# The last pair's 3x3 convolution by four products for two columns, first statistics ahead of the other weights, and a new order in the last layers

## The chip, the cores and the metric

The kernel runs on one core of a Trainium2 chip. The metric is device time in microseconds (us), the median of several executions. A profile is taken of one further execution. The engines are TensorE (PE, matmuls; its weight loads are listed as PEld), VectorE (DVE), ScalarE (ACT), GpSimd (POOL) and SyncE (SP, which here only issues DMAs). All data are 32-bit floats; every matmul of the program is recorded as two MATMUL instructions.

## What is computed

Four residual layers on x of shape (8, 64, 128, 128), each of the form x = x + layer(groupnorm(x)) with 32 groups of two channels:

```python
x = x + _L0_conv_ref(_gn(x), ...)   # 3x3 "adder" convolution: relu(b - sum |patch - w|)
x = x + _L1_conv_ref(_gn(x), ...)   # per channel: silu and a cubic spline
x = x + _L2_conv_ref(_gn(x), ...)   # Haar transform, convolutions, gelu, inverse transform
x = x + _L3_conv_ref(_gn(x), ...)   # nearest of 512 embeddings of 64 channels, per pixel
```

Layer 2 makes four half-size images of each image (256 channels of 64x64), transposes them, and applies a depthwise 3x3 convolution, a 1x1 convolution, a 3x3 convolution (256 to 256 channels), gelu and the inverse transform. Layer 3 takes, for every pixel, the embedding row with the smallest squared distance.

## The kernel before

Two images make a pair: 64 channels of each fill the 128 partitions. Four pairs are worked through. The first layer (`layer0`) is by far the longest; it makes |x - w| tiles on ACT and DVE and sums them over channels on PE (L691). While it runs for pairs 1 to 3, the layers 2 and 3 of the pair before run beside it (`layer2_beside`, `layer3_beside`), a little at every step. `layer0` issues PE, ACT and DVE instructions in an order written out by hand. Everywhere else a scheduler orders each engine's queue: program order is the priority, and an instruction is taken when the scheduler believes its inputs and buffers ready. At run time every queue, SP's of DMAs too, is worked strictly in the order chosen.

**Setup** (`setup`, L193 to L362) prepares all weights. For layer 2 it transposes the 3x3 weights (L304), multiplies them by the 1x1 weights (wp, L318) so that both convolutions become one 3x3 convolution w2 of shape 128 x 4 x 9 x 2 x 128, and stores it to DRAM (L321). gp (L335) and gam hold what the 1x1 bias gives through the 3x3 taps; `edge` makes the small tensors that correct it at the image's borders. After setup, `run` calls `raw_norm(0)`: eight tiles of pair 0 are loaded with three buffers (L403), their statistics are taken (L419), the group norm is formed, the first chunk of x is loaded into x0 (L500) and normalized (L485). Then `layer0` begins.

**The last pair** has no layer 0 to hide behind: its layers 1, 2 and 3 run alone at the end, in eight chunks of 16 image rows.

`layer1` loads its data, and, for the last pair, w2 from DRAM into SBUF in four parts (L799).

`layer2` works a chunk in these steps. `transform` forms the four Haar images on DVE (L840 to L846). `border` copies border rows between neighbouring chunks on POOL (L833, L834), for the Haar images and for the depthwise result. `depthwise` makes nine taps for each of four channel groups k on DVE (L857 the first tap, L859 the other eight). `convolve`, once for each half of the output channels (oab), multiplies nine taps x four k x two images on PE (L873), each a 64 x 128 weight by 64 x 512 columns; the two images use the upper and the lower half of the PE rows. Border corrections are small matmuls (L877). gelu goes over the 1024 columns on ACT (L879). `inverse` of the chunk before, between the two convolves, makes four positions on PE (L888), which DVE adds to x (L890), and takes statistics. The loop keeps the depthwise work one chunk ahead; a chunk can be convolved only when the depthwise result of the next chunk has given it its border row.

`layer3` works a chunk by normalizing it (L485), squaring it on ACT (L926), summing squares over channels on PE (px, L929, 16 matmuls with two columns each), and then for each of 16 rows and both images: the products with the embeddings on PE (L938), ACT's distance part t (L941), DVE's difference and maximum (L944) and its index (L946), and a gather of the embedding rows by POOL (L947). Each row's gathered values are then transposed on PE (q, L955); after four rows DVE adds them to x (L958). The chunk is stored at its end.

Of the kernel before, what the change touches and what calls it, by code (L numbers as in the profile page):

```python
# [100 lines left out]
class Net:  # L101
    def __init__(self, ctx, tc, x, w0, b0, coef, sbase, ssp, bias1, dw_w, dw_b, pw_w, pw_b, cv_w, cv_b, embed, out):
# [9 lines left out]
        self.x_of = [self.dram.tile([P, H * W], F32, name=f"x{n}_dram") for n in range(3)]  # L112
        self.setup(w0, b0, coef, sbase, ssp, bias1, dw_w, dw_b, pw_w, pw_b, cv_w, cv_b, embed)
# [6 lines left out]
    def setup(self, w0, b0, coef, sbase, ssp, bias1, dw_w, dw_b, pw_w, pw_b, cv_w, cv_b, embed):  # L120
# [66 lines left out]
        with tc.tile_pool(name="setup", bufs=1) as sp, tc.tile_pool(name="setup_ps", bufs=2, space=PSUM) as pp:  # L187
# [13 lines left out]
            for n in range(len(PLANS)):  # L201
# [7 lines left out]
                nc.vector.tensor_tensor(self.b0[:, n], ws, braw, ALU.add)  # L209

# [112 lines left out]


# [39 lines left out]
    def edge(self):  # L364
# [14 lines left out]
        for n in range(2):  # L379
# [8 lines left out]
            nc.vector.tensor_tensor(self.edge_r[n][:, HW2 - 1 : HW2], sums[:, 1:2], one[:, row[2] : row[2] + 1], ALU.subtract)  # L388

# [308 lines left out]
    def layer1(self, mr, stats, nxt):  # L698
# [3 lines left out]
        with ExitStack() as ctx:  # L702
# [49 lines left out]
            for n in range(2 * NCH):  # L752
# [44 lines left out]
                if n in range(4, 12, 2) and nxt is None:  # L797
                    k = n // 2 - 2
                    nc.sync.dma_start(out=self.w2[:, k], in_=self.w2_dram[:, k])  # L799
# [4 lines left out]
    def layer2(self, mr, stats):  # L804

# [7 lines left out]
        with ExitStack() as ctx:  # L813
            sp = ctx.enter_context(tc.tile_pool(name="l2", bufs=1))
            pp = ctx.enter_context(tc.tile_pool(name="l2_ps", bufs=2, space=PSUM))
            pi = ctx.enter_context(tc.tile_pool(name="l2_pi", bufs=1, space=PSUM))
# [6 lines left out]
            def padded(name, bufs, j):  # L823
                t = sp.tile([P, 4, G + 2, S + 2], F32, name=name, tag=name, bufs=bufs)
                nc.gpsimd.memset(t[:, :, :, 0 : S + 2 : S + 1], 0.0)
                if j == 0:
                    nc.gpsimd.memset(t[:, :, 0, 1 : S + 1], 0.0)
                if j == NCH - 1:
                    nc.gpsimd.memset(t[:, :, G + 1, 1 : S + 1], 0.0)
                return t  # L830

            def border(above, below):
                nc.gpsimd.tensor_copy(above[:, :, G + 1, 1 : S + 1], below[:, :, 1, 1 : S + 1])  # L833
                nc.gpsimd.tensor_copy(below[:, :, 0, 1 : S + 1], above[:, :, G, 1 : S + 1])  # L834

            def transform(j):
                t = padded("sub", 2, j)
                xv = self.x[j]
                s, d = (sp.tile([P, R, S], F32, name=n) for n in ("hs", "hd"))
                nc.vector.tensor_tensor(s, xv[:, :, 0:W:2], xv[:, :, 1:W:2], ALU.add)  # L840
                nc.vector.tensor_tensor(d, xv[:, :, 0:W:2], xv[:, :, 1:W:2], ALU.subtract)
                at = (slice(1, G + 1), slice(1, S + 1))
                nc.vector.scalar_tensor_tensor(t[:, 0, at[0], at[1]], s[:, 0:R:2], m4, s[:, 1:R:2], ALU.add, ALU.add)
                nc.vector.tensor_tensor(t[:, 1, at[0], at[1]], s[:, 0:R:2], s[:, 1:R:2], ALU.subtract)
                nc.vector.tensor_tensor(t[:, 2, at[0], at[1]], d[:, 0:R:2], d[:, 1:R:2], ALU.add)
                nc.vector.tensor_tensor(t[:, 3, at[0], at[1]], d[:, 0:R:2], d[:, 1:R:2], ALU.subtract)  # L846
                return t

            def depthwise(j, sub):
                t = padded("dw", 3, j)  # L850
                for k in range(4):
                    out = t[:, k, 1 : G + 1, 1 : S + 1]
                    for n, (di, dj, w) in enumerate(taps):
                        v = sub[:, k, di : di + G, dj : dj + S]
                        wt = dws[:, k, w : w + 1]
                        if n == 0:
                            nc.vector.tensor_scalar(out, v, wt, self.dwb[:, k : k + 1], ALU.mult, ALU.add)  # L857
                        else:
                            nc.vector.scalar_tensor_tensor(out, v, wt, out, ALU.mult, ALU.add)  # L859
                return t  # L860

            def convolve(j, dw, oab):
                ps = pp.tile([P, 2, G, S], F32, name="ps")
                ends = [(slice(0, G), slice(0, S, S - 1), self.edge_c)]
                if j == 0:
                    ends.append((0, slice(0, S), self.edge_r[0]))
                if j == NCH - 1:
                    ends.append((G - 1, slice(0, S), self.edge_r[1]))
                for n, (di, dj, w) in enumerate(taps):
                    for k in range(4):  # L870
                        for i, rows in enumerate(images):
                            v = dw[rows, k, di : di + G, dj : dj + S]
                            nc.tensor.matmul(ps[:, i], self.w2[rows, k, w, oab, :], v, start=(n == 0 and k == 0), stop=(n == 8 and k == 3))  # L873
                    if n == 0:
                        for r, c, e in ends:
                            for i, rows in enumerate(images):
                                nc.tensor.matmul(ps[:, i, r, c], self.gam[rows, oab, :], e[rows], start=False, stop=False)  # L877
                g = sp.tile([P, 2, G, S], F32, name="g", tag="g", bufs=4)
                nc.scalar.activation(g.rearrange("p i r c -> p (i r c)"), ps.rearrange("p i r c -> p (i r c)"), AF.Gelu, bias=self.b2c[:, oab : oab + 1])  # L879
                return g  # L880

            def inverse(j, gs):
                py = pi.tile([P, 4, G, S], F32, name="py")
# [420 lines left out]
```

## Time and profile before

| | us |
|---|---|
| median of 3 runs | 19244.84 (19237.88 to 19248.91) |
| the profiled execution: time / span | 19248.76 / 19247.0 |
| PE busy | 18582.4 (97%) |
| DVE busy | 17869.9 (93%) |
| ACT busy | 17302.3 (90%) |
| POOL busy | 2775.6 (14%) |
| granted PE clock, mean | 0.977 |

Where the stages lie in the span (us from its start):

| stage | from | to |
|---|---|---|
| setup (its last ACT instruction ends) | 0 | 98.6 |
| raw tiles, statistics and x0 of pair 0 | 98 | 133.4 |
| layer 0 of all pairs, with the rest beside it | 133.4 | 17913 |
| last pair, layer 1 | 17913 | 18172 |
| last pair, layer 2 (first L873 matmul at 18237.02) | 18172 | 18804 |
| last pair, layer 3 | 18804 | 19247 |

Durations of the rows that the change touches, from the profile's groups (mean of one, ns): L873 597, L859 744, L857 569, L888 605, L890 689, L879 1114, L938 1017, L929 353, L955 420, L944 678, L946 684, L947 958. Matmuls overlap, two with 64 rows each run side by side, and DVE's instructions overlap at their ends, so that the distance from one start to the next is shorter than these means; where that matters it is read from starts in the trace.

How to read it: a busy engine is not an engine at its peak. The chain of waits follows what ended last back through what released it; the windows give busy times, the granted clock (1.00 is full) and the DMA share for a stretch of time. An engine's idle time counts only where that engine, or one that waits for it, is the bound of the stage.

### The profile page before, as it was taken

Reading aid. Unit: us, or ns where it says so; the run is one execution under the profiler, and the core shown is the slowest. Engines: PE = TensorE matmul, PEld = TensorE weight load, DVE = VectorE, ACT = ScalarE, POOL = GpSimd, SP = SyncE. Lnnn points to the kernel's source line nnn. Section 1 sums busy time; section 2 is a strip of 40 time slices with the busy share of each in tenths; the row PEclk is TensorE's granted clock in tenths of the full one; section 3 lists DMA queues with packets and bytes.
Section 4 is the critical chain, followed back from the end, with each engine's and each line's share of the span. In section 5 each row is a group of like instructions: output and inputs, shape, how many; then the busy total and the mean of one; then the engine's idle time right before and its main releaser. Section 6 shows DMA issues by size and latency. Waiting matters only on the chain.

```text
span 19247.0 us, 328577 instructions
## 1 busy us (share of the span) xinstructions
PE 18582.4 (97%) x145850; PEld 5795.2 (30%) x145850; DVE 17869.9 (93%) x13785; ACT 17302.3 (90%) x6401; POOL 2775.6 (14%) x1698
## 2 busy tenths in 40 slices
PE   8999999999999999999999999999999999999898
PEld 2333233233233222222223222222232322222343
DVE  8999999989999999998999999998899999999837
ACT  7999999889999999988999999998999999999603
POOL 0000000000000344200000034420000004441005
PEclk9999999999999999999999999999999999999996
DMA  1000000121111000021111100002011110000101
GB/s 52 6 11 10 6 12 8 43 63 37 36 33 37 20 20 27 26 73 35 34 41 35 33 15 24 24 28 82 28 33 38 35 33 19 23 22 16 59 1 35
DMA packets 412639, 584.02 MB, mean 30 GB/s; under 512 B 64080, under 2 KB 309456, under 8 KB 385744
## 3 DMA queue, kind: packets, MB, share of 16 engines
q1 hardware_dynamic: 355408, 497.90, 8.6%
q0 software_dynamic: 55808, 65.11, 1.9%
q8 instruction: 1142, 18.71, 0.4%
q14 instruction: 281, 2.30, 0.0%
HBM read 439.55 MB, written 123.25 MB: 29 GB/s over the span
## 4 chain that ended last, share of the span: by engine, by line
PE 54%; DVE 27%; issue 9%; ACT 8%; DMA 1%; POOL 0%; SPq 0%; DVEq 0%; ACTq 0%; POOLq 0%
PE ps L691 39%; DVE buf L624 12%; DVE buf L628 9%; ACT buf L622 7%; PE cv L1066 5%; PE pa L787 2%; PE pb L787 2%; PE ps L873 2%; DVE dw L1043 1%; DVE ix L1193 1%; DVE nd L1191 1%; PE ps L938 1%; DVE x L624 1%; PE py L1089 1%; PE pd L1179 1%
## 5 line engine op out<-in xcount | busy, mean ns | idle before, releaser
L691 PE MATMUL ps<-buf,sel 128*32 128x512 f32 x116336 | 13032.1, 598 | 358.4 <-DVE buf L628 233.4
L622 ACT ACTIVATE buf<-buf,w 128x4096 f32<-128x4096 f32 x1980 | 7212.9, 3708 | 305.9 <-PE ps L691 299.5
L622 ACT ACTIVATE buf<-x,w 128x4096 f32<-128x4096 f32 x1938 | 7044.5, 3708 | 376.5 <-PE ps L691 290.8
L691 PEld LDWEIGHTS ps<-buf,sel 128*32 128x32 f32 x116336 | 3642.9, 110 | 9338.4 <-issue 7867.1
L624 DVE TENSOR_SCALAR buf<-buf,w 128x4096 f32<-128x4096 f32 x1795 | 4162.7, 2357 | 193.7 <-PE ps L691 192.9
L624 DVE TENSOR_SCALAR buf<-x,w 128x4096 f32<-128x4096 f32 x1558 | 3640.1, 2367 | 284.3 <-PE ps L691 274.5
L628 DVE SCALAR_TENSOR_TENSOR buf<-buf,w,buf 128x2048 f32<-128x2048 f32 x1262 | 2913.5, 2349 | 23.0
L628 DVE SCALAR_TENSOR_TENSOR buf<-x,w,buf 128x2048 f32<-128x2048 f32 x1072 | 2475.3, 2349 | 19.7
L1194 POOL DMA_INDIRECT g<-in_L_conv_embed_weight,ix x768 | 1825.6, 2377 | 2849.3 <-issue 1432.4
L602 POOL DMA_DIRECT2D y<-in_x x480 | 608.3, 2072 | 9442.6 <-ACT y L589 6467.9
L1066 PE MATMUL cv<-dw,w2s 64*128 64x512 f32 x6912 | 1655.2, 607 | 3.3 <-issue 3.3
L622 ACT ACTIVATE x<-buf,w 128x4096 f32<-128x4096 f32 x396 | 1468.6, 3709 | 60.8 <-PE ps L691 60.7
L691 PE MATMUL ps<-x,sel 128*32 128x512 f32 x10832 | 1302.8, 595 | 27.1 <-DVE x L628 18.9
L1066 PEld LDWEIGHTS cv<-dw,w2s 64*128 64x128 f32 x6912 | 628.0, 186 | 1025.4 <-issue 1012.0
L624 DVE TENSOR_SCALAR x<-buf,w 128x4096 f32<-128x4096 f32 x281 | 660.2, 2349 | 24.4 <-PE ps L691 24.2
L691 PEld LDWEIGHTS ps<-x,sel 128*32 128x32 f32 x10832 | 352.6, 110 | 849.1 <-issue 742.7
L1043 DVE SCALAR_TENSOR_TENSOR dw<-sub,dws,dw 128x512 f32<-128x512 f32 (+2 forms) x768 | 574.9, 749 | 10.6
L873 PE MATMUL ps<-dw,w 64*128 64x512 f32 x2304 | 525.5, 597 | 29.4 <-DVE dw L859 20.4
L1191 DVE CUSTOM_DVE_ANT_0 nd<-pd,t 128x512 f32<-128x512 f32 x768 | 520.0, 677 | 30.5 <-ACT t L1181 30.4
L1193 DVE FIND_INDEX8 ix<-best,nd 128x8 uint32<-128x512 f32 x768 | 526.1, 685 | 0.1
L776 DVE TENSOR_TENSOR r<-r,r 128x1024 f32<-128x1024 f32 x384 | 455.0, 1219 | 76.1 <-ACT r L775 76.1
L1179 PE MATMUL pd<-embT,xn 64*128 64x512 f32 x1536 | 491.4, 650 | 30.0 <-DVE best L1191 29.6
(220 smaller groups left out, 7961.3 us busy)
## 6 DMA issues: line engine op xcount, KB each, us to landing
w2s<-w_dram SPq DMA_DIRECT2D x576, 192.0 KB
xd<-x_dram SPq DMA_DIRECT2D x256, 256.0 KB
x<-x_dram SPq DMA_DIRECT2D x56, 1024.0 KB
raw<-in_x SPq DMA_DIRECT2D x32, 1024.0 KB
x_dram<-y SPq DMA_DIRECT2D x512, 64.0 KB
out<-x SPq DMA_DIRECT2D x32, 1024.0 KB
y<-in_x POOLq DMA_DIRECT2D x480, 64.0 KB, 4.2
x_dram<-x SPq DMA_DIRECT2D x24, 1024.0 KB
```

The source lines that it names most:

```text
L622: nc.scalar.activation(ab, tap(j, ts[0]), AF.Abs, bias=w[:, ts[0] : ts[0] + 1], scale=-1.0)
L624: nc.vector.tensor_scalar(ab, tap(j, ts[0]), w[:, ts[0] : ts[0] + 1], None, ALU.max)
L628: nc.vector.scalar_tensor_tensor(at, tap(j, t, h), w[:, t : t + 1], at, ALU.max, ALU.add)
L691: nc.tensor.matmul(at, sel[:, M - 1 - m : 3 * M - 1 - m], rhs, start=(n == first[p]), stop=(n + 1 == first[p + 1]))
L787: nc.tensor.matmul(to[images[i], q, :], dspl[:, k, ws[i], :], cubes[i][:, cols], start=(p == 0), stop=stop)
L873: nc.tensor.matmul(ps[:, i], self.w2[rows, k, w, oab, :], v, start=(n == 0 and k == 0), stop=(n == 8 and k == 3))
L1043: nc.vector.scalar_tensor_tensor(out, v, wt, out, ALU.mult, ALU.add)
L1066: nc.tensor.matmul(ps[:, i], weights[r, w // 3, :], v, start=(k == 0 and n == 0), stop=(k == 3 and n == 8))
L1179: nc.tensor.matmul(ps, xns[j][at, r, :], self.embT[at, :], start=True, stop=True)
L1191: nc.vector.tensor_tensor_reduce(nd, ps, t, 1.0, -FAR, ALU.subtract, ALU.max, mx[:, 0:1])
L1193: nc.vector.max_index(ix, mx, nd)
L1194: nc.gpsimd.indirect_dma_start(out=g[:, img, :], out_offset=None, in_=self.embed, in_offset=bass.IndirectOffsetOnAxis(ap=ix[:, 0:1], axis=0),)
```

## The change

**Setup.** The statistics of pair 0, the load of x0 and its normalization move from `run` into `setup`, to just behind the first layer's weights; x0 is allocated before setup. Behind the store of w2, setup computes u2 from it and stores that to DRAM too (128 x 2 x 4 x 4 x 3 x 128). `edge` makes two more small tensors, negated borders. The load of w2 into SBUF during layer 1 goes.

**Layer 2 of the last pair.** The three taps along the image's columns are replaced by a scheme that forms two neighbouring output columns from four products instead of six. Its input side v (four combinations of columns, made on DVE from the depthwise result) has half the columns; the weights u2 are combinations of the three taps. Four products m0 to m3 are accumulated over k and three row taps, each with 256 columns for each image; the outputs are m0 + (m1 + m2) for even and (m1 - m2) - m3 for odd columns, formed by one ACT copy and four DVE operations before gelu. The weights of each product are loaded from DRAM as they are needed (four buffers). The first depthwise tap goes to ACT. A chunk's Haar rows now reach two rows into the next chunk, so that a chunk's depthwise result needs no row from the next one. PSUM is divided anew: three buffers of two banks for products (before: two) and two of one bank for the inverse (before: one of four).

**Layer 3.** Chunk j + 1 is normalized and its squares are summed when row 6 of chunk j is due, its sums taken at row 12; the four transposes and the add of a group of rows come six rows later than its last row.

```diff
             nc.sync.dma_start(out=self.w2_dram, in_=w2)
+            self.u2_dram = self.dram.tile([P, 2, 4, 4, 3, P], F32, name="u2_dram")
+            for k in range(4):
+                u = sp.tile([P, 2, 4, 3, P], F32, name="u2", tag="u2")
+                g = [w2[:, k, 3 * dj : 3 * dj + 3].rearrange("p d o n -> p o d n") for dj in range(3)]
+                nc.scalar.copy(u[:, :, 0], g[0])
+                nc.scalar.copy(u[:, :, 3], g[2])
+                nc.vector.tensor_tensor(u[:, :, 1], g[0], g[2], ALU.add)
+                nc.vector.tensor_tensor(u[:, :, 2], u[:, :, 1], g[1], ALU.subtract)
+                nc.vector.tensor_tensor(u[:, :, 1], u[:, :, 1], g[1], ALU.add)
+                nc.vector.tensor_scalar(u[:, :, 1:3], u[:, :, 1:3], 0.5, None, ALU.mult)
+                for o in range(2):
+                    nc.sync.dma_start(out=self.u2_dram[:, o, :, k], in_=u[:, o])
...
+            pp = ctx.enter_context(tc.tile_pool(name="l2_ps", bufs=3, space=PSUM))
+            pi = ctx.enter_context(tc.tile_pool(name="l2_pi", bufs=2, space=PSUM))
...
+                        if n == 0:
+                            nc.scalar.activation(out, v, AF.Identity, bias=self.dwb[:, k : k + 1], scale=wt)
+                        else:
+                            nc.vector.scalar_tensor_tensor(out, v, wt, out, ALU.mult, ALU.add)
+                d = [t[:, :, :, n : n + S - 1 : 2] for n in range(4)]
+                v = sp.tile([P, 4, 4, G + 2, S // 2], F32, name="v", bufs=2)
+                nc.vector.tensor_tensor(v[:, :, 0], d[0], d[2], ALU.subtract)
+                nc.vector.tensor_tensor(v[:, :, 1], d[1], d[2], ALU.add)
+                nc.vector.tensor_tensor(v[:, :, 2], d[2], d[1], ALU.subtract)
+                nc.vector.tensor_tensor(v[:, :, 3], d[1], d[3], ALU.subtract)
+                return v
...
+                for m in range(4):
+                    if m % 2 == 0:
+                        pair = pp.tile([P, 2, 2, G, S // 2], F32, name="m")
+                    ps = pair[:, :, m % 2]
+                    u2 = sp.tile([P, 4, 3, P], F32, name="u2", tag="u2", bufs=4)
+                    nc.sync.dma_start(out=u2, in_=self.u2_dram[:, oab, m])
                     for k in range(4):
+                        for di in range(3):
                             for i, rows in enumerate(images):
+                                nc.tensor.matmul(ps[:, i], u2[rows, k, di, :], v[rows, k, m, di : di + G, :], start=(k == 0 and di == 0), stop=(k == 3 and di == 2))
...
+                m1, a, b = (sp.tile([P, 2, G, S // 2], F32, name=n) for n in ("m1", "ma", "mb"))
+                nc.scalar.copy(m1, ms[1])
+                nc.vector.tensor_tensor(a, ms[2], m1, ALU.add)
+                nc.vector.tensor_tensor(b, m1, ms[2], ALU.subtract)
+                nc.vector.tensor_tensor(g[:, :, :, 0:S:2], ms[0], a, ALU.add)
+                nc.vector.tensor_tensor(g[:, :, :, 1:S:2], b, ms[3], ALU.subtract)
...
+            for j in range(NCH):
                 done = dw
+                if j + 1 < NCH:
+                    transform(j + 1)
+                    dw = depthwise(j + 1)
+                gs = [convolve(j, done, 0)]
+                if late is not None:
+                    inverse(*late)
+                gs.append(convolve(j, done, 1))
+                late = (j, gs)
             inverse(*late)
...
+            for n in range(NCH * R + LATE):
+                j, r = divmod(n, R)
+                if j + 1 < NCH and r in (6, 12):
+                    (prepare if r == 6 else take_squares)(j + 1)
+                if j < NCH:
+                    nearest(j, r)
+                if n >= LATE + 3 and (n - LATE - 3) % 4 == 0:
+                    add(*divmod(n - LATE - 3, R))
```

## The prediction

> **What bounds the kernel now.** I read the chain of waits first, then the windows by stage, then the groups and waits of the stages that the change touches. Nearly all of the span (137 to 17913 us) is the first layer with the other pairs' layers beside it, and no instruction in it changes. Three stretches at the two ends do change, and the chain runs through all three.
>
> The start, from the chain of waits (start us, us, what):
> ```profile
> 85.04 7.93 PE gp L335 x36
> ...
> 97.96 4.68 DMA raw<-in_x
> ...
> 116.95 13.80 DMA x<-in_x
> ...
> 130.85 2.56 DVE x L485
> ...
> 133.48 3.72 ACT buf L622
> ...
> 137.25 22.87 PE ps L691 x192
> ```
> All weights are prepared first (to 98.6); only then come pair 0's raw tiles, their statistics and the first chunk of x, so that the first matmul of layer 0 starts at 137.25.
>
> The last pair's layer 2, from the chain there and from the windows (us; busy time of PE, PEld, DVE, ACT, POOL; granted clock; DMA):
> ```profile
> 18234.49 2.48 POOL dw L833
> 18237.02 14.81 PE ps L873 x56
> 18252.22 30.97 PE ps L873 x144
> 18283.31 27.57 PE ps L873 x128
> ```
> ```profile
> 18400.00:18600.00 200.00, 200.00 (x918) 87.03 (x916) 83.34 (x128) 5.65 (x6) 4.94 (x14) 1.00 0.00 1
> ...
> 18980.00:19034.00 54.00, 50.45 (x114) 20.70 (x114) 45.31 (x135) 23.30 (x34) 30.96 (x33) 0.56 0.13 40
> ```
> From 18237 to 18786 PE never rests, and DVE has half its time free: the 3x3 convolution is the bound. A convolve is 72 products, each recorded as two 512-column matmuls, the two images side by side: 144 records in 30.97 us, so 72 slots of 0.43 us (0.427 over the 288 records from 18321.5 to 18383.1). PE starts only at 18237 because two chunks must be depthwise-convolved before the first border is whole. The second row is one chunk of layer 3: DVE 45.3 of 54 us. Its idle time there, by the waits of that chunk:
> ```profile
> DVE nd L944 <- PE ps L938: 4.6, 1, 4.6
> DVE x L958 <- PE q L955: 4.1, 4, 1.3
> ```
> The 4.6 is PE doing the sums of squares of the next chunk (px, 6.9 us) ahead of products; the 4.1 are four adds whose transposes wait for a row's gather.
>
> **Part 1, the first statistics ahead of the other weights.** The chain from 97.96 to 133.48 (raw loads, statistics, x0, normalize) leaves; what stays is the weight chain, 38.8 (cvn lands) to 98.6, 59.8 us, then the first ACT tile 3.72. New at the front of SP's queue are pair 0's raw loads and x0, with their waits on the statistics (eight tiles, 2.5 us of DVE each); cvn stands behind them. If cvn still lands at 38.8, layer 0 starts at 102.3: 35 us won. If all raw and x0 traffic goes first (97.96 to 130.75, so 32.8 us, from 16.3 on, then cvn's 5.75), cvn lands at 55 and layer 0 starts at 118.5: 19 won. The u2 stores add 6.3 MB beside w2's 4.7 MB, which took 12.5 us (85.47 to 97.96), and layer 0's buffers may lie under w2 and u2: last u2 about 4 us after the last w2, then two stores together about 15 us, 104.5 instead of 98.6, so 6 less. Another 8 us go if pair 1's three raw tiles (3 MB), hoisted already now, go first too. The ends are 35 won and, with a late SP wait on top, 5 lost; I take **18 won**, near the later arrival, since program order puts the raw tiles first. The u2 arithmetic (per k two ACT copies and four DVE operations of 768 to 1536 columns; 0.58 us for 512 on ACT, 1.21 for 1024 on DVE) lies beside wp matmuls of 8 us per k, where DVE is idle; without that cover it would cost 16 us.
>
> **Part 2, layer 2.** Removed per convolve: 72 products of 512 columns. Added: 4 x 12 x 2 = 96 products of 256 columns, so 96 slots. What a slot costs hangs on the weight loads, which now come twice as often. Nearest row by columns: gp, 128x256, new weights in each of 36 records in 7.93 us, 0.22 us each. Nearest by tiling: the border matmuls of 64 rows with 16 or 64 columns, their loads one after the other:
> ```profile
> 18757.75 0.19 PEld L877 LDWEIGHTS ps<-edge_c,gam 64*128 64x128 f32 x1 [0.24 <-issue]
> 18757.75 0.18 PEld L873 LDWEIGHTS ps<-dw,w 64*128 64x128 f32 x1
> 18757.86 0.19 PEld L877 LDWEIGHTS ps<-edge_r,gam 64*128 64x128 f32 x1
> 18757.86 0.19 PEld L873 LDWEIGHTS ps<-dw,w 64*128 64x128 f32 x1
> 18757.97 0.19 PEld L877 LDWEIGHTS ps<-edge_r,gam 64*128 64x128 f32 x1
> ```
> Both row groups load at the same moment, every 0.11 us, less than the 0.213 of a 256-column slot. Ends: 0.213 (half of 0.427) and 0.40 (0.213 + 0.19, nothing overlapped). I take 0.22, by gp. The Trainium skill speaks against this: "TensorE: Matmul & The Clock Gate", Part 3, says that a weight load overlaps running matmuls only if its row group differs, and the same page's rule for loads (columns / 1.2) gives 107 ns for 128 columns. By that a slot would be 0.32, a convolve 31 us and the whole 19187. The gp row, full array and 0.22 a record, does not follow it.
>
> Convolve: 96 x 0.22 = 21.1, and four border slots of 0.11, 21.6 us. Sixteen: 16 x (30.96 - 21.6) = 149.8 won. The inverse held PE for 4 x 1.87 = 7.5 us a chunk; with two py buffers four positions of 4 slots x 0.427 = 6.8: 7 x 0.7 = 5 won. A chunk on PE is 2 x 21.6 + 6.8 = 50 us.
>
> Does DVE keep up? Pitches from its timeline: 32 taps of 0.664 = 21.2 (the first tap of each k goes to ACT, which is idle); hs/hd and sub in two parts 6.6 with the halo copy; v, four operations of 1280 columns at 1.13 per 1024, 5.7; combining, 8 x 0.69 = 5.5; adds 2.8; statistics 2.5. Sum 44 against PE's 50: DVE fits, tightly. Three m buffers give the combining about 10 us (half a convolve) before PE needs a bank back. In the first round they don't suffice: DVE is in chunk 1 for 33 us while PE is done with the first convolve after 21.6; 4 us lost there, and I allow 6 for waits like it.
>
> Start of the layer: scales at 18181.6, the second part of transform about 2 us, the first ACT tap 0.7, then 32 taps over 9 rows, 0.664 x 576/512 = 0.75 each, 23.9, and v 5.7: 18214.4 instead of 18237.0, **22.6 won**. Tail: after the last convolve, one ACT copy and four DVE operations, 3.3 lost. Weights: 64 x 2 loads of 786 KB, 6.3 MB per 50 us or 126 GB/s, alone on SP's queue then, with four buffers (over 40 us ahead); the start moved 391 GB/s, so they are hidden. If not, PE waits for them directly. The w2 loads that layer 1 loses stood beside a PE with 20.00 of 20 us busy: nothing. The two edge tiles: three DVE operations of 0.15 us, hidden in the setup. Layer 2: 149.8 + 5 + 22.6 - 10 - 3.3 = **164 won**.
>
> **Part 3, layer 3.** The transposes come six rows later, so that the 4.1 us per chunk of waits for gathers go: 8 x 4.1 = 33. The px burst stays as one block, and with it the 4.6. PE is late next: at clock 0.56 to 0.59 a row of products takes 2.07 us, 16 x 2.07 + 6.9 + 16 x 0.42 = 46.7 per chunk against DVE's 45.3, and four transposes now stand in one block of 1.7 us ahead of products. Ends: 70 won (all 8.7 us of DVE idle per chunk) and 20 lost (four uncovered blocks, 4 x 1.7 = 6.8 for 4.1 saved). I take **30 won**. On the clock the skill (same page, Part 1) says that PE drops to half rate after an idle window of 3.4 us and returns after a busy one. If fewer waits kept it at full rate, px would halve and up to 8 x 3.5 = 28 us more would go; the 0.59 in every chunk, with PE 92% busy, says that it mostly doesn't.
>
> **Sum**, against the profiled execution's 19248.76 (span 19247.0): 18 + 164 + 30 = 212, so 19036.8. That execution stands 3.9 above the median of the three, so the forecast is **19033**.
>
> **Rivals.** (a) DVE's order holds PE back: 44 of 50 us leaves little room, and depthwise of the next chunk stands ahead of the combining in program order. With 60 us per chunk, 8 x 10 = 80 less: 19113. For it: DVE did the chunks ahead in one block from 18183 to 18270. Against it: the adds of the inverse stood between such blocks where their data came.
> (b) Strict program order: DVE does 33 us of the next chunk, then combining, adds, combining behind PE; 66 us a chunk, 128 less: 19161.
> (c) All gaps close, start 35 and layer 3 70: 57 more, 18976. For it: DVE alone needs only 45.3 a chunk, and cvn could land as now.
> (d) Slower: weight loads are not overlapped in the new slots, 0.40 each. Convolve 38.9, 16 x 17.3 = 277 lost: 19310. It decides from 0.36 a slot on (212 / 16 / 96 = 0.14 above 0.22). Against it are gp and the border loads.
> (e) The change does not do what it says: the new waits (u2, m buffers, v) eat what the products save, PE idles a third of layer 2, and the time stays within 0.2% (about what a measurement can tell from no change) of 19245.
>
> **How the numbers follow.** Forecast 0.66 (19033, own range 18990 to 19080 from the ends of the start and of layer 3), (a) 0.14, (b) 0.05, (c) 0.09, (d) 0.03, (e) 0.03. Faster by over 0.2%: 0.66 + 0.14 + 0.05 + 0.09 = 0.94; within: 0.03; slower: 0.03. The range takes in (a) and (c), 18975 to 19115; (b), (d), (e) and some tails, about 2 in 10, stay out.
>
> **What would show it.** Part 1: first layer-0 matmul near 119, raw loads before cvn in SP's queue. Part 2: 192 records of 256 columns in 21 us, first at about 18196 (18214 less 18), PE without gaps from chunk 2 on, layer 3 beginning near 18622. A slot over 0.25 proves (d)'s mechanism, PE idle before m matmuls with DVE as releaser (a) or (b). Part 3: no DVE wait on q, still one of 4 to 5 us on ps per chunk, some 50 us a chunk. The prediction fails if DVE becomes the bound of layer 2, or if PE at half clock becomes that of layer 3.

## The result, and the profile after

The changed kernel takes 19155.08 us (19149.18 to 19157.30), the kernel before 19244.84: a ratio of 0.9953, 95% interval [0.9943, 0.9964]. The gain is 90 us where 212 were forecast, and the time lies above the whole range. The profiled execution took 19149.18, its span is 19147.4 us. By stages, each read from the first instruction of the next in the two traces (us):

| stage | before | changed | difference | forecast |
|---|---|---|---|---|
| to the first matmul of layer 0 | 137.25 | 143.70 | +6.4 | -18 |
| from there to the last add of layer 0 | 17774.7 | 17764.8 | -9.9 | 0 |
| last add to the first Haar operation of layer 2 (mostly layer 1) | 257.9 | 259.1 | +1.2 | 0 |
| layer 2 | 634.3 | 554.5 | -79.9 | -164 |
| layer 3 | 442.9 | 425.4 | -17.5 | -30 |
| span | 19247.0 | 19147.4 | -99.6 | -212 |

No code of the second row changes. Over the fourteen traces of this study, all with the same code there, it took 17761 to 17780 us, so a difference of 10 says nothing, and small effects below are read from their own stage and not from the total.

Lines of the changed kernel: layer 0's matmul is L722 and its ACT tile L653; in layer 2 the products m are L918, v L900 to L903, the taps L897, the combination L932 to L935, gelu L937, the inverse py L946 and its add L948; in layer 3 px is L985, ps L997, nd L1003, the transposes q L1016, their add L1018.

**The start.** The chain of waits of the changed kernel (start us, us, what):
```profile
26.53 10.71 DVE stats L450 x18
...
38.32 7.64 SPq L233
...
62.00 5.43 DMA cvn<-in_L_conv_cv_w
...
114.17 15.84 DMA u_dram<-u
...
134.55 5.27 DMA u_dram<-u
139.93 2.42 ACT buf L653
```
Raw loads and x0 no longer stand between the weights and layer 0, as meant. But the statistics and SP's first small load behind the raw loads (cf, L233) now stand ahead of the convolution's weights, which come late (the last load of cvn is issued at 67.4, before at 38.8). From these the chain runs on to the end, there twice through a store of u2: the last of four sets of u2 can be formed only when the store of an earlier one has left their only buffer, and that store stands behind the 4.7 MB one of w2. Layer 0's first ACT tile waits for the second store, because its buffer lies where u2 was.

**Layer 2.** The windows of the changed kernel (us; busy time and, in brackets, instructions of PE, PEld, DVE, ACT, POOL; granted clock; DMA share; GB/s), two chunks in the steady state, the last chunks, and one chunk of layer 3:
```profile
18348.00:18412.00 64.00, 49.69 (x402) 38.10 (x400) 39.41 (x61) 6.28 (x8) 0.61 (x1) 0.87 0.31 99
18412.00:18475.00 63.00, 51.73 (x438) 40.71 (x438) 39.62 (x59) 6.29 (x8) 0.61 (x1) 0.92 0.32 101
18570.00:18640.00 70.00, 70.00 (x594) 54.23 (x592) 23.33 (x32) 4.62 (x5) 0.00 (x0) 1.00 0.38 120
18843.00:18895.00 52.00, 39.29 (x110) 17.24 (x112) 43.84 (x133) 22.73 (x33) 30.39 (x32) 0.65 0.14 41
```
Before, PE was busy 200 of 200 us here. Now neither PE nor DVE is full in a chunk of 63 to 67 us, while at the end, where no depthwise work is left, PE is full again. Two engines that both rest may be waiting for each other. PE's waits over layer 2 (us in total, times, longest):
```profile
PE py L946 <- DVE x L948: 59.6, 4, 27.4
PE m L918 <- issue: 31.4, 2, 18.6
...
PE py L946 <- ACT g L937: 2.0, 1, 2.0
```
93 us of waits behind its first product (the 28.1 for the first v, left out, belong to the layer's start). "Issue" means that the trace names no releaser. What DVE does meanwhile, from its timeline in one chunk (start us, us, instruction, and in brackets the idle time before it and what ended it):
```profile
18366.21 0.69 DVE L932 TENSOR_TENSOR ma<-m,m 128x512 f32<-128x512 f32 x1 [18.22 <-PE m L918]
...
18368.61 1.48 DVE L900 TENSOR_TENSOR v<-dw 128x1280 f32<-128x1280 f32 x1
...
18375.24 21.33 DVE L897 SCALAR_TENSOR_TENSOR dw<-sub,dws,dw 128x512 f32<-128x512 f32 x32 [0.95 <-ACT dw L895]
...
18402.04 0.68 DVE L932 TENSOR_TENSOR ma<-m,m 128x512 f32<-128x512 f32 x1
...
18404.43 1.28 DVE L948 TENSOR_TENSOR x<-x,py 128x512 f32<-128x512 f32 x2
```
DVE has worked ahead until both buffers of v are full, idles 18.2 us for the second convolve to end, then does the combination, the next v, 32 taps and the Haar operations in one block, 36 us long. Only behind that block come the next combination and the adds of the inverse, for which PE has meanwhile stopped.

A product's cost was as forecast (start us, us, x records of 256 columns):
```profile
18682.49 15.79 PE L918 MATMUL m<-v,u 64*128 64x256 f32 x144
```
15.79 / 72 = 0.219 us a slot (the two images side by side), 21.06 for the 96 of a convolve.

**Layer 3.** DVE's waits there, changed kernel:
```profile
DVE nd L1003 <- PE ps L997: 49.7, 13, 6.3
...
DVE x L1018 <- PE q L1016: 3.7, 1, 3.7
```
Before, these two stood at 32.3 us (7 times) and 34.7. The waits for gathered rows are gone but one; the stall at each px burst but the first (4.9) has grown from 4.6 to 6.3 us, and a wait of 0.9 to 1.9 us just ahead of it has joined it.

### The profile page after: what moved, and what is told of

Read it like the earlier page. It is cut to its first block, busy times and chain, and to the rows that moved or that the text cites. A ratio compares the mean times of both kernels' runs of the same rounds, so it can differ in the third digit from the quotient of the medians.

```text
span 19147.4 us, 330733 instructions
## 1 busy us (share of the span) xinstructions
PE 18332.0 (96%) x146698; PEld 5818.3 (30%) x146698; DVE 17951.2 (94%) x13918; ACT 17340.8 (91%) x6457; POOL 2778.2 (15%) x1663
## 4 chain that ended last, share of the span: by engine, by line
PE 53%; DVE 28%; issue 10%; ACT 8%; DMA 1%; SPq 0%; POOL 0%; DVEq 0%; ACTq 0%; POOLq 0%
PE ps L722 39%; DVE buf L655 12%; DVE buf L659 9%; ACT buf L653 7%; PE cv L1139 5%; PE pa L818 2%; PE pb L818 2%; DVE dw L1116 1%; DVE nd L1264 1%; DVE ix L1266 1%; DVE dw L897 1%; PE py L1162 1%; DVE x L655 1%; ACT t L1254 1%; PE pd L1252 1%
## 5 line engine op out<-in xcount | busy, mean ns | idle before, releaser
L722 PE MATMUL ps<-buf,sel 128*32 128x512 f32 x116336 | 13030.5, 597 | 371.1 <-DVE buf L659 234.2
L653 ACT ACTIVATE buf<-buf,w 128x4096 f32<-128x4096 f32 x1980 | 7213.9, 3710 | 301.8 <-PE ps L722 295.3
L653 ACT ACTIVATE buf<-x,w 128x4096 f32<-128x4096 f32 x1938 | 7046.2, 3710 | 347.0 <-PE ps L722 288.0
L722 PEld LDWEIGHTS ps<-buf,sel 128*32 128x32 f32 x116336 | 3625.9, 110 | 9365.5 <-issue 7898.4
L653 ACT ACTIVATE x<-buf,w 128x4096 f32<-128x4096 f32 x396 | 1468.9, 3709 | 59.3 <-PE ps L722 59.3
L722 PE MATMUL ps<-x,sel 128*32 128x512 f32 x10832 | 1303.0, 594 | 27.1 <-DVE x L659 18.5
L722 PEld LDWEIGHTS ps<-x,sel 128*32 128x32 f32 x10832 | 350.8, 110 | 851.1 <-issue 747.5
L1252 PE MATMUL pd<-embT,xn 64*128 64x512 f32 x1536 | 490.1, 650 | 29.1 <-DVE best L1264 28.7
L1254 ACT ACTIVATE t<-esq_half,xsq 128x512 f32<-128x512 f32 x768 | 510.8, 717 | 3.1 <-DVE best L1264 3.1
```

The source lines that it names most:

```text
L653: nc.scalar.activation(ab, tap(j, ts[0]), AF.Abs, bias=w[:, ts[0] : ts[0] + 1], scale=-1.0)
L722: nc.tensor.matmul(at, sel[:, M - 1 - m : 3 * M - 1 - m], rhs, start=(n == first[p]), stop=(n + 1 == first[p + 1]))
L1252: nc.tensor.matmul(ps, xns[j][at, r, :], self.embT[at, :], start=True, stop=True)
L1254: nc.scalar.activation(t, self.esq_half, AF.Identity, bias=xsqs[j][:, n : n + 1])
```

## Experiments

**Layer 2: VectorE's order, the buffers, or the weights?** The work ahead becomes a generator (`steps`) and is taken in pieces, two of them ahead of each add in `inverse`; buffers and work stay as they are.
```diff
+            ctx.enter_context(tc.manual_schedule(engines={ET.PE, ET.Activation, ET.DVE}))
...
             for j in range(NCH):
+                ahead, v = steps(j + 1), vs.pop(j)
+                ms = convolve(j, v, 0)
+                take(ahead, 16)
+                gs = [combine(ms, 0)]
+                if late is not None:
+                    inverse(*late, ahead)
+                ms = convolve(j, v, 1)
+                take(ahead, 40)
+                gs.append(combine(ms, 1))
```


> The changed kernel, with layer 2's order on TensorE, ScalarE and VectorE written out: the depthwise taps of the next chunk are cut into pieces, and each combination of four products and each addition of the inverse stands between two pieces instead of behind the whole block. The work, the two buffers of v, the three of the products and the streamed weights stay as they are. In the changed kernel layer 2 took 554.5 us (18167.6 to 18722.0), two steady chunks 67 and 62.7 us. Theory 'order' (PE's 121 us of idle time in that layer all end with a VectorE instruction that stood behind some 30 us of work for a later chunk): a steady chunk falls to PE's own 50 to 53 us, PE's waits on the additions fall from 59.6 us to under 15, the two unnamed stalls of 12.8 and 18.6 us go, and the layer takes 455 to 480 us, 75 to 100 less. Rival 'buffers' (two buffers of v and three of the products are too few, whatever the order): the chunk stays at 60 us or more, and the layer loses under 20 us. Rival 'weights' (the streamed weights come late, which the two stalls without a named releaser could be): the two stalls stay, the layer takes 520 us or more.

Layer 2 took 458.3 us, 96 less, and the whole 19057.5. (6 of the 96 only moved: the first Haar operation comes 265.2 us after the last add of layer 0, not 259.1. From that add to layer 3 it is 90.) A window of it, and PE's waits on adds:
```profile
18300.00:18400.00 100.00, 97.54 (x846) 77.93 (x844) 87.39 (x129) 12.80 (x16) 3.88 (x2) 1.00 0.38 123
```
```profile
PE py L950 <- DVE x L953: 6.6, 6, 1.1
```
A chunk is 51.2 us (from one convolve's first border matmul, 18356.94, to the same one a chunk later, 18408.16), and DVE is busy 87 of 100 us where it had 40 of 63. With the buffers unchanged, "buffers" is out.

The same with only DVE's order written out, `engines={ET.DVE}`:

> As the kernel with layer 2's order written out, but for VectorE's alone: TensorE's and ScalarE's orders are left to the scheduler. With all three written out layer 2 fell from 554.5 to 458.3 us. Theory 'VectorE's order' (only the position of the combinations and additions in VectorE's queue mattered): 455 to 475 us here as well. Rival 'all three' (it took TensorE's or ScalarE's order too, say a gelu or a first tap behind a copy that waits): over 490 us.

Layer 2 took 452.1 us, PE 50.00 busy of 50 in six windows in a row. With the queues of the other two engines left to the scheduler, VectorE's order in its queue is enough. (Layer 3 took 440.4 us in that run, which is taken up below.)

The weights loaded once:
```diff
+            u2s = []
...
-                    u2 = sp.tile([P, 4, 3, P], F32, name="u2", tag="u2", bufs=4)
-                    nc.sync.dma_start(out=u2, in_=self.u2_dram[:, oab, m])
+                    if len(u2s) < 4:
+                        u2s.append(sp.tile([P, 4, 3, P], F32, name=f"u2_{m}"))
+                        nc.sync.dma_start(out=u2s[m], in_=self.u2_dram[:, oab, m])
+                    u2 = u2s[m]
```


> The changed kernel, but layer 2's convolution loads its transformed weights only once, for the four products of the first output half, and uses these for both halves and all eight chunks: 60 of the 64 loads on SP's queue are left out (the second half's output is then of the wrong weights). Rival 'weights': the stalls of 12.8 and 18.6 us in layer 2 that name no releaser go, 31 us or more off its 554.5. Theory 'order': nothing in layer 2 moves by more than 5 us, since both stalls end 0.2 to 0.4 us after the combination's third instruction, which reads the product's buffer that is wanted.

Layer 2 took 554.5 us, unmoved. (This kernel leaves out the weights of the second output half.) With the loads out of the way the trace also names the releaser of the two stalls, DVE's combination (g, L938 in this kernel):
```profile
PE py L950 <- DVE x L952: 59.5, 4, 27.3
PE m L922 <- DVE g L938: 31.4, 2, 18.6
```
So PE waited there for a product's buffer that the combination had still to read, behind DVE's taps, and streaming the weights cost nothing here.

**The start: the stores, and the move.**
```diff
-            nc.sync.dma_start(out=self.w2_dram, in_=w2)
...
-                u = sp.tile([P, 2, 4, 3, P], F32, name="u2", tag="u2")
+                u = sp.tile([P, 2, 4, 3, P], F32, name="u2", tag="u2", bufs=2)
...
                 for o in range(2):
                     nc.sync.dma_start(out=self.u2_dram[:, o, :, k], in_=u[:, o])
+            nc.sync.dma_start(out=self.w2_dram, in_=w2)
```


> The changed kernel, with two buffers instead of one for the transformed weights in the setup, and the 4.6 MB store of the old weights put behind their stores on SP's queue. In the changed kernel the first matmul of layer 0 stands at 143.70 us, the setup's own last ScalarE instruction ends at 125.8, and VectorE and ScalarE wait 11.6 and 8.3 us on the stores of u. Theory 'store' (the single buffer's stores, queued behind the large one, end the start's chain): the first matmul comes at 129 to 132 us, some 12 to 14 us earlier, and all that follows moves by as much. Rival 'weights late' (the chain is set by the weights' loads, which the statistics' loads push back from 38.8 to 67.4 us, and the stores only fill a wait that is there anyway): first matmul within 4 us of 143.70.

The first matmul came at 134.65, 9.1 us earlier, not 12 to 14. ACT's timeline in this kernel shows why:
```profile
125.59 0.60 ACT L381 ACTIVATE esq_half<-ep 128x512 f32<-128x512 f32 x1 [1.93 <-PE ep L379]
130.88 21.74 ACT L651 ACTIVATE buf<-x,w 128x4096 f32<-128x4096 f32 x6 [4.69 <-DMA u_dram<-u]
```
One store still stands between, and ACT waits 4.7 us for it. The span was 19147.1, as if nothing had been won: the middle happened to take 8 us more. The second half of the expectation, that all that follows moves as much, fell with that.

The statistics back behind the setup, u2 kept:

> The changed kernel, but with the first pair's statistics, its first chunk and that chunk's normalization back where they were, behind the setup; the transformed weights and the rest of the change stay. Theory 'the move pays, the transformed weights take it back': before the change the first matmul of layer 0 stood at 137.25; the transformed weights' two copies, four additions and stores come on top of that chain and cost 12 to 20 us, so it stands at 150 to 157 here, 6 to 13 us later than with the statistics ahead (143.70). Rival 'the move costs' (loads of the weights 28.7 us later, and nothing won): first matmul at 143 us or earlier. The middle of the run (the end of layer 0 in each pair, relative to the first) gained about 10 us in the changed kernel though none of its code was changed; if that is a matter of chance between executions, it takes another value here and in the other runs of this call.

The first matmul came at 150.07. So u2 cost 12.8 us of the old start (137.25), and the move won 6.4 of it back (143.70; the other seven kernels with the same setup have 143.9 to 146.3, so 4 to 6). With the statistics behind, the stretch that ends the start is again theirs (SP, then ACT):
```profile
112.56 18.45 SPq L430 DMA_DIRECT2D raw<-in_x  x8
```
```profile
146.30 7.32 ACT L649 ACTIVATE buf<-x,w 128x4096 f32<-128x4096 f32 x2 [42.08 <-DVE x L512]
```

**Layer 3: the gathers or the burst?** First, layer 3's old code in the changed kernel:

> The changed kernel with layer 3 as it was before: the squares' sums at the head of each chunk, the transposes in the program beside their own row. Part 3 alone is undone. If part 3 is independent of the rest, layer 3 goes from 425.4 us back to 441 to 445 and layer 2 stays at 554.5; if the 17.5 us came from something else (the clock that layer 2 leaves behind), layer 3 stays below 435.

446.5 us, with layer 2 at 555.5: by this trace and the kernel before, part 3 by itself is worth some 17 to 21 us. (Against the 440.4 above it would be 6; the last section comes back to this scatter.) Then TensorE's order in layer 3 as the program has it:
```diff
+            ctx.enter_context(tc.manual_schedule(engines={ET.PE}))
             xns, pxs, xsqs, gs = {}, {}, {}, {}
```


> The changed kernel with TensorE's order of layer 3 as the program writes it: four transposes at a time, six rows and more behind their gathers, and the 32 small matmuls px still in one burst. In the changed kernel's profile a transpose stands beside each row, waits 3.65 to 4.22 us on the gather just ahead of each px burst, and VectorE then waits 6.3 us on ps, about once a chunk (44.9 us in all). Theory 'gather' (the transposes that wait take away the lead with which TensorE enters the burst): the wait on ps shrinks to 0 to 3 us a chunk and layer 3 takes 395 to 412 us. Rival 'burst' (7 us of px are longer than any lead that four product buffers allow): the wait stays at 4 to 6 us a chunk, layer 3 at 413 to 425.

A miss for both theories: 468.6 us, 43 longer. Waits of DVE, and of PE:
```profile
DVE xsq L990 <- PE px L986: 62.3, 7, 9.1
DVE nd L1004 <- PE ps L998: 17.8, 9, 4.2
```
```profile
PE px L986 <- ACT sq L983: 56.2, 6, 12.1
```
The wait on ps did fall, but the program places px directly behind the square that it reads, and in that place PE holds everything back for ACT. The scheduler had moved px to a later place. The experiment brought in a wait of its own and decides nothing. So px was spread, from row 6 on, two of its sixteen at each row:
```diff
-                if j + 1 < NCH and r in (6, 12):
-                    (prepare if r == 6 else take_squares)(j + 1)
+                if j + 1 < NCH:
+                    if r == 4:
+                        prepare(j + 1)
+                    if r == 15:
+                        take_squares(j + 1)
                 if j < NCH:
                     nearest(j, r)
+                    if j + 1 < NCH and 6 <= r < 14:
+                        sum_squares(j + 1, 2 * (r - 6), 2 * (r - 5))
```


> As the kernel with TensorE's order written out, and the px matmuls of the next chunk besides spread over eight rows, four at each. VectorE's own work is 44.5 us in a chunk of 52, so the floor of a chunk is some 45 us. Theory 'gather' and theory 'burst' both expect the wait on ps to vanish here, 45 to 47 us a chunk, layer 3 at 378 to 395; what tells them apart is how much of it the kernel with the burst left whole has won already. Rival 'clock' (TensorE, with 40 us of work in a chunk at a granted clock of 0.65, is the bound as soon as the gaps close): waits on ps spread over all rows, chunk 49 or more, layer 3 above 405.

408.0 us, 17 less than the changed kernel, but above the 378 to 395 of both theories and past the 405 that the rival 'clock' named: that rival is not out. And the same with the burst whole at row 10 (`if r == 10: sum_squares(j + 1, 0, R)`):

> The changed kernel with TensorE's order of layer 3 written out (four transposes at a time, six rows behind), the squares begun two rows earlier, and the px matmuls in one burst, four rows later than in the kernel whose px waited 56 us on ScalarE's squares, so that the squares are there when the burst comes. It differs from the kernel with spread px (layer 3 in 408.0 us) only in the burst. Theory 'gather' (the transposes that waited took TensorE's lead; with them out of the way it enters the burst with four products ready): waits of VectorE on ps around the burst of 0 to 3 us, layer 3 within 408 to 418 us. Rival 'burst': each burst of 7 us costs VectorE 4 to 5 us beyond the spread kernel's, seven times, layer 3 at 430 to 445.

420.3 us, between the two. DVE's waits on PE, spread and burst:
```profile
DVE nd L1007 <- PE ps L1001: 8.7, 10, 2.1
DVE nd L1007 <- PE px L989: 7.9, 6, 4.1
```
```profile
DVE nd L1007 <- PE ps L1001: 24.1, 9, 4.7
DVE nd L1007 <- remote: 5.3, 1, 5.3
```
The second line of the burst kernel is one of its seven bursts too, whose releaser the trace does not name. Its seven waits at bursts are 2.7 to 5.3 us, 28.7 in sum, 4.1 each, against some 7.5 (6.3 and about 1.2 ahead of it) in six of the changed kernel's seven. By these waits both theories hold a part: transposes that wait beside their row would cost 3 us or so of each stall, and the burst itself up to 4. That is argued, not shown. The spread kernel waits too, 16.6 us in the two lines above, and the kernels e8 and e10 below, spread as well, take 418.8 and 419.2 us in layer 3, with 22 and 31 us of DVE's waits on ps and px. What the spread itself is worth against the burst stays open.

**The mends together, and the start once more.** e8 is the by-hand order of layer 2, the stores and the spread px in one kernel:

> The changed kernel with three mends together: layer 2's order written out on TensorE, ScalarE and VectorE; two buffers for the setup's transformed weights with the large store behind theirs; layer 3 with TensorE's order written out and the px matmuls spread over eight rows. If the three add up, the changed kernel's stages lose 96 us in layer 2 (554.5 to 458), 17 in layer 3 (425 to 408) and 9 ahead of the first matmul of layer 0 (143.7 to 134.7): 19025 to 19045 us, a ratio of 0.988 to 0.9895 to the kernel before. Rival 'clock' (TensorE, fuller in layer 2, is granted less in layer 3): layer 3 stays above 415 us, and the whole at 19045 or more.

19050.6 us, ratio 0.9893 [0.9876, 0.9909]: layer 2 458.1, first matmul 136.3, layer 3 418.8. The first two add up; layer 3 does not, and the total is 6 us above what was expected. Both numbers of the rival 'clock' came, over 415 and over 19045, but not its reason: the mean clock in layer 3 was 0.64, against 0.60 in the kernel of 408.0 us. With DVE's order alone in layer 2:

> As the kernel with the three mends, but in layer 2 with VectorE's order alone written out. With all three engines' orders written out layer 2 took 458.3 us and layer 3 after it 424.6 at a granted clock of 0.65 to 0.69; with VectorE's alone 452.1 and 440.4 at 0.60 to 0.64, though layer 3's own order was the same in both. Theory 'clock follows the load' (TensorE without any gap in layer 2, 50.0 us busy of 50 against 48.8, is granted less in layer 3): layer 3 is 8 us or more longer here than in the kernel with the three mends, at a lower clock. Rival 'chance': within 4 us of it, or shorter.

Layer 2 454.1 and layer 3 419.2 us, 0.4 from the kernel with all three orders written. That is what "chance" expected: a layer 2 without gaps did not by itself bring a longer layer 3. What lay behind the 440.4 above stays open. Last, the statistics behind the loads of the other weights:
```diff
-            self.mr0 = self.mr_tile()
-            for _ in self.raw_norm(0, self.mr0):
-                pass
-            self.load_chunk(0, 0, self.x0)
-            self.pad_first(self.mr0)
...
                             nc.sync.dma_start(out=b2[rows, n, ab : ab + 1], in_=bv[k])
+            self.mr0 = self.mr_tile()
+            for _ in self.raw_norm(0, self.mr0):
+                pass
+            self.load_chunk(0, 0, self.x0)
+            self.pad_first(self.mr0)
             cvt = sp.tile([P, 2, 9, 2, P], F32, name="cvt")
```


> The kernel with the three mends, and the first pair's statistics one step later in the setup: behind the loads of the other weights instead of ahead of them (still ahead of all the work on these weights). The statistics' loads took 21 us of SP's queue, so the last of the convolution's weights landed at 67.4 us instead of 38.8, and the chain from there (transposes, products, transformed weights, stores) ended the start at 134.7 to 136.3 with the stores mended. Theory 'weights late' (that chain is the start's bound, and the statistics have room beside it: they end 24 us after their last load and would end near 75 to 90): the last weights' load stands at 38 to 43 us, and the first matmul of layer 0 comes at 106 to 122. Rival 'VectorE' (the statistics' 21 us of VectorE and the wait for each load fall among the copies that feed the chain's transposes, and give back what the earlier load wins): first matmul at 126 or later. The whole follows the start: 14 to 30 us under the 19050.6 of the kernel with the three mends, if the middle of the run, which took 14116 to 14135 us over the traces so far, does not cover it.

The first matmul came at 118.72. SP's queue and ACT's first tile:
```profile
40.01 0.47 SPq L295 DMA_DIRECT2D cvn<-in_L_conv_cv_w  x1
...
41.80 25.81 SPq L431 DMA_DIRECT2D raw<-in_x  x8
```
```profile
114.96 10.92 ACT L650 ACTIVATE buf<-x,w 128x4096 f32<-128x4096 f32 x3 [4.49 <-DMA u_dram<-u]
```
The weights' chain starts 28 us earlier and the statistics run beside it; a store of u2 still ends it. The whole took 18998.8 us, ratio 0.9871 [0.9855, 0.9888], the lowest time of the study, 52 us under e8 where 14 to 30 were expected. Of the 43 us between the profiled spans (19041.8 and 18998.6) the start gave 17.6, the middle took 6.5 back, and 32 came from layer 3, whose order is the same in both; the last section leaves open why.

## Why the prediction was wrong, point by point

**Part 2, the slot: right.** 0.219 us for 0.22, the products of a convolve 21.06 for 21.1. The 190 ns loads, one for every record, were hidden, and rival (d) is out. The rule that the prediction weighed from the Trainium skill ("TensorE: Matmul & The Clock Gate", Part 3: a weight load overlaps running matmuls only if its row group differs) would have made the slot 0.32, by the prediction's estimate; the measured 0.219 decides against it for this pattern. The streamed weights were hidden, as forecast (the trace has 64 loads, 8 a chunk, not "64 x 2"; its 6.3 MB a chunk is right).

**Part 2, "does DVE keep up": the step that failed.** DVE's work, 44 us a chunk, was right (40 to 44 measured), and so was PE's 50 (51.2 with the order mended). The failing term is the allowance "4 us lost there, and I allow 6 for waits like it": PE waited 93 us, of which 31.4 at the products' buffers and 59.6 at the adds. That is 83 us more than allowed; layer 2 missed its 164 by 84, and the stretch from its first to its last product by 95 (next point). The prediction compared amounts of work, where the order in one queue decided. It named the mechanism as rival (a), priced it at 80, and gave it 0.14; "the adds of the inverse stood between such blocks where their data came" was read from the kernel before, where PE was late and DVE always had time. The mended order, 90 us less, shows that nothing but the order stood in the way: from the last add of layer 0 to layer 3 it then takes 169 us less than before, more than the 164.

**Part 2, its ends.** The first product came 36.9 us after the first Haar operation, for 67.2 before: 30.3 won, 22.6 forecast. The tail cost 0.3 more, 3.3 forecast. From the first product to the end of the last, 548.8 us became 499.0, 49.8 less for a forecast of 144.8. The 95 missing there are the 83 of waits and some 12 more, which fit the clock of 0.87 and 0.92 in the steady chunks; that second share was not tested by itself.

**Part 1: both terms mis-sized.** The stores were put at 6 and u2 cost 12.8, much of it through the single buffer and the place of the stores (mending both took 9.1 off the changed kernel's start). The prediction's own later arrival gives 19, less these 6, so 13; its 18 is not worked out from them. Read net of the 6, it leaves 24 for the move, which won 6.4: cvn came 28.7 us later, not 16, and the chain from it to layer 0 is the bound. The estimate of 16 put cvn directly behind the raw loads; the small loads of other weights, with their waits, stand between in SP's queue and take 21.4 us there (46.0 to 67.4; before, 22.5, from 16.3 to 38.8). Loads in the other order gave 17.6 us more, which shows that step.

**Part 3: direction right, size off.** "The px burst stays as one block, and with it the 4.6": it cost 4.9 in the first chunk and some 7.5 in each of the next six. The waits for gathers left DVE's adds, as forecast (34.7 to 3.7 us), but came back in part at PE, where the scheduler left a transpose beside each row, not four in a block, and PE waited 86.4 us for gathered rows; that this took PE's lead ahead of the burst is argued from the kernel with the burst at row 10. 17.5 won, 30 forecast. Layer 3 of one and the same order differed by up to 32 us between kernels, as the last section shows, so the 17.5 is loose; the stall at the burst, 6.3 us at its longest in the 440.4 us too, is the firmer measure.

**Rivals.** (a) is what happened in layer 2. Its 19113 missed because part 1 added 24 us and part 3 12.5 to it. (b) comes near in number (66 us a chunk, 19161), and in the two chunks shown, 67 and 63 us long, DVE's queue has its order: a block of the next work, a combination, the adds, and after a rest the second combination. But (b) has this from strict program order and in every chunk; here the scheduler had worked a chunk further ahead, until both v buffers were full, and the last chunks ran at 50. (c), (d) and (e) fell.

## What to carry to other kernels

When a change makes the bound engine faster, add up not only the work of the next engine but also the longest block in its queue that stands ahead of what the fast engine waits for; 44 us of work in a 50 us chunk cost 93 us of waits over the eight chunks because 36 of them came in one piece. Two engines that both rest in a stage point to order, and cutting the long block into pieces tests it with all buffers unchanged. Of something moved to the front of a queue, price what it pushes back by the whole time that the queue then stands, waits included, and try the order in which the long chain's loads go first.

## What the runs showed of the hardware

Layer 3 with spread px, with one and the same order of instructions on every engine, took 408.0, 418.8, 419.2 and 386.7 us in four kernels (e7, e8, e10, e11). Executions of one kernel agree far better: the four of e8 took 19043.5 to 19051.7 us, the four of e11 18990.9 to 19001.2. One window of e8 and one of e11:
```profile
18700.00:18800.00 100.00, 88.14 (x221) 40.79 (x222) 89.27 (x268) 46.39 (x66) 62.11 (x64) 0.60 0.16 43
```
```profile
18740.00:18840.00 100.00, 93.29 (x255) 43.52 (x256) 97.13 (x292) 49.38 (x72) 68.20 (x71) 0.62 0.15 45
```
The means of the clock hardly differ, but DVE is busy 89 of 100 us in one and 97 in the other: in the slower one it stops now and then for 3 to 4 us, where products and px run at the low clock one after the other (2.08 us for a row's products and 1.01 for its px, against DVE's 2.7 a row). Which stretches meet the low clock may decide; that is argued, not shown. The same layer 3 as in the changed kernel took 424.6 to 426.5 us in five traces and 440.4 in a sixth, at a clock of 0.60 to 0.64 instead of 0.65 to 0.69. The Trainium skill ("TensorE: Matmul & The Clock Gate", Part 1) says that the window in which PE's activity is judged runs freely and that the point of change therefore varies from run to run. A difference that stays over four executions each does not look like such a variation, and no run here shows the window itself. The chip is an open rival: e8 and e10, 0.4 us apart, and e9 with its 420.3 ran on one chip, e7 and the kernel of 440.4 on a second, e11 on a third, and four of the five from 424.6 to 426.5 on a fourth. The kernel before, run on all four, took 19243.4 to 19253.8 us there, 10 apart; none of the variants was run on two of them.

A small load behind large ones was slow to issue: the first load of cf took 7.64 us of SP's queue behind raw loads and x0 (7.6 to 9.1 in the eleven kernels with that order), and 0.51 us with nothing large ahead of it, in the kernel with the statistics behind.
